# One transformer step on a Trainium2 core: the first modulation alone at the front, and attention's addend made from the second norm's result

## The chip, the core and the metric

The kernel runs on one core of one Trainium2 chip. Its engines are TensorE (PE in the profile, with PEld for its weight loads), VectorE (DVE), ScalarE (ACT), GpSimd (POOL) and SyncE (SP), which issues most DMAs. The metric is the device time of one execution in microseconds (us). Everything is float32.

## The reference

The input x is 16 sequences of 128 tokens with 128 features. Four residual sublayers follow one another: an adaptive-norm transformer block (self-attention, cross-attention to a context of 77 tokens, a gated feed-forward), a mixture of experts with a shared expert, a slot attention of three turns, and a second mixture of experts. Each sublayer gets a plain layer norm of the running sum and is added to it. The change touches the start of the first sublayer alone:

```python
def adaln(x, t, w, b):
    emb = t @ w + b
    scale, shift = jnp.split(emb, 2, axis=-1)
    return layernorm(x) * (1.0 + scale) + shift
...
h1 = adaln(x, t, norm1_w, norm1_b)
x = mha(h1, h1, attn1_wq, attn1_wk, attn1_wv, attn1_wo, attn1_bo) + x
h2 = adaln(x, t, norm2_w, norm2_b)
x = mha(h2, context, attn2_wq, attn2_wk, attn2_wv, attn2_wo, attn2_bo) + x
h3 = adaln(x, t, norm3_w, norm3_b)
x = glu_ff(h3, ff_w1, ff_b1, ff_w2, ff_b2) + x
```

The x of this block is already layernorm(x) of the input, so h1 needs the norm of a norm. With v the variance of the input, the first norm divides by sqrt(v + eps), and the norm of that divides x - mean by sqrt(v(1 + eps) + eps^2). Both come from one set of statistics. t is one vector per sequence (cond), so there are 16 scales and 16 shifts for each of the three norms: the three modulations.

## The kernel before, in words

All sixteen sequences stay in SBUF: x0 is the input, r the running sum of the first sublayer, each 128 tokens on the partitions by 16 x 128. Attention works in groups of two sequences: groups 0 to 7 are self-attention, 8 to 15 cross-attention. The code is written in program order; a scheduler then sets the order of the instructions on each engine, and each engine runs its own list in that order. An instruction that waits holds everything behind it on its engine.

The loads (lines 111 to 125) are all issued from SP's queue in the order of the code: the first two sequences of x0, the columns of biases (cols_sb), condT, normw (the weights of all three modulations, 384 KB), the two weights of self-attention (wa0 for query and key, wa1 for value and output), the rows of biases spread over all partitions (brow, srow), the other x0 in seven loads, the context, and the rest. From the ninth load on, a load also waits on SP for the one eight places before it.

The modulations (lines 152 to 157) come first in the code: per norm, two matmuls of a 128x128 block of normw with condT into a PSUM tile pe, and two DVE instructions that make ada_sc (1 + scale) and ada_sh (shift).

attn_norm (line 250) makes a group's norm. For self-attention: variance (statistics sti, and the small steps dmi, qqi, mvi on 128x2), two small DVE steps that write the two variances into q (lines 261 and 262, tile qjj), POOL's power to -0.5 (rsqrt, line 170, tile yj), and then normalize (line 217) twice, two DVE instructions each: z (tile za) for the attention, and r, the plain norm of x, which is the addend of the residual. At last POOL adds the output bias to r (row_add, line 244, from brow). z has two buffers, the small tiles six each; r has a place of its own for every sequence and waits for none.

attn_prologue (line 272) transposes z on PE (ta), has ACT apply the modulation (ha, line 281), and projects queries, keys (pq, line 298, copied by ACT at line 299) and values (pv, line 314). scores (line 339) multiplies queries by keys for eight heads into a PSUM tile s of which there are two buffers, and on DVE takes the maximum (mx, line 363), subtracts it (e, line 365, which frees the buffer), on ACT the exponential, on DVE the sum and its reciprocal (lines 368 and 369), and on POOL the multiplication by it (line 370). attend_t transposes e (te, line 380), attend_v multiplies it with the values, attn_project applies the output weights (ya) and adds the result into r (line 404). The loop over units (one sequence of one group each) starts the next group's prologue before a group's first unit, and runs a unit's scores one unit ahead. The projections of a group and its values use the same two PSUM buffers (psM, tag "mm") as the modulations.

Of the kernel before, what the change touches and what calls it, by code (L numbers as in the profile page):

```python
# [14 lines left out]
ALU = mybir.AluOpType  # L15
# [3 lines left out]
P = 128  # L19
B = 16  # L20
D = 128
# [8 lines left out]
LN_EPS = 1e-5  # L30
# [26 lines left out]
def pixart_kernel(  # L57
# [18 lines left out]
    V, S, G, PE = nc.vector, nc.scalar, nc.gpsimd, nc.tensor  # L76
# [15 lines left out]
    normw = attc.tile([P, 6, D], F32, name="normw")  # L92
    ctxT = attc.tile([P, B * NC], F32, name="ctxT")
    brow = const.tile([P, 9, D], F32, name="brow")
# [7 lines left out]
    dma = nc.sync.dma_start  # L102
# [3 lines left out]
    def load_w(src, n, name):  # L106
        t = wpool.tile([P, n], F32, name=name, tag="w")
        dma(out=t, in_=src)
        return t
# [1 line left out]
    dma(out=x0[:, 0:2, :], in_=xr[:, 0:2, :])  # L111
    dma(out=cols_sb, in_=cols)
    dma(out=condT, in_=cond_t)
    dma(out=normw, in_=norm_w.rearrange("p (k d) -> p k d", d=D))
    w_att = [load_w(attn_w[0], 2048, "wa0"), load_w(attn_w[1], 2048, "wa1")]
    dma(out=brow, in_=rows[0, 0 : 9 * D].partition_broadcast(P).rearrange("p (k d) -> p k d", d=D))
    dma(out=srow, in_=rows[0, R_SMALL * D : N_ROWS].partition_broadcast(P))
    for b in range(2, B, 2):
        dma(out=x0[:, b : b + 2, :], in_=xr[:, b : b + 2, :])
    dma(out=ctxT, in_=ctx_feat)  # L120
    w_att += [load_w(attn_w[2], 2048, "wa2"), load_w(attn_w[3], 2048, "wa3")]
# [24 lines left out]
    def col(i, p=P):  # L146
        return cols_sb[:p, i : i + 1]
# [1 line left out]

    ada_sc = const.tile([P, 3, B], F32, name="ada_sc")  # L150
    ada_sh = const.tile([P, 3, B], F32, name="ada_sh")
    for k in range(3):
        pe = psM.tile([P, 2, B], F32, name=f"ada{k}", tag="mm")
        for j in range(2):
            PE.matmul(pe[:, j, :], lhsT=normw[:, 2 * k + j, :], rhs=condT, start=True, stop=True)
        V.tensor_scalar(ada_sc[:, k, :], pe[:, 0, :], col(C_NORM + 2 * k), 1.0, ALU.add, ALU.add)
        V.tensor_scalar(ada_sh[:, k, :], pe[:, 1, :], col(C_NORM + 2 * k + 1), None, ALU.add)
# [5 lines left out]
    def small(nm, tag, p, n, lane):  # L163

        return sm.tile([P, 4], F32, name=f"{tag}{nm}", tag=f"{tag}{lane}", bufs=6 if lane == "" else 2)[:p, :n]

    def rsqrt(v, p, n, nm, lane):

        y = small(nm, "y", p, n, lane)
        G.tensor_tensor(y, v, mhalf[:p, :n], ALU.pow)  # L170
        return y
# [43 lines left out]
    def normalize(dst, src, rs, mean, n):  # L215
        for i in range(n):
            V.tensor_scalar(
                dst[:, i, :], src[:, i, :], mean[:, i : i + 1], rs[:, i : i + 1], ALU.subtract, ALU.mult
            )
# [15 lines left out]
    def transpose_n(z, p, n, nm, g=0):  # L235

        t = psT.tile([P, 4, P], F32, name=f"t{nm}", tag=t_tag(g))
        for i in range(n):
            PE.transpose(t[:, i, :p], z[:, i, :], ident[:p, :p])
        return t  # L240

    def row_add(ap, k, n):

        G.tensor_tensor(ap, ap, brow[:, k, :].unsqueeze(1).to_broadcast([P, n, D]), ALU.add)


    GB = 2
    GT = GB * P

    def attn_norm(g):  # L250

        ph, gi = divmod(g, B // GB)
        b0 = gi * GB
        rg = r[:, b0 : b0 + GB, :]
        z = zp.tile([P, 4, D], F32, name=f"za{g}", tag="z")
        if ph == 0:

            xg = x0[:, b0 : b0 + GB, :]
            v, mean = variance(xg, P, GB, f"i{g}")
            q = small(f"j{g}", "qj", P, 4, "")  # L260
            V.tensor_scalar(q[:, GB:], v, 1.0 + LN_EPS, LN_EPS * LN_EPS, ALU.mult, ALU.add)
            V.tensor_scalar(q[:, :GB], v, LN_EPS, None, ALU.add)
            rs = rsqrt(q, P, 2 * GB, f"j{g}", "")
            normalize(z, xg, rs[:, GB:], mean, GB)
            normalize(rg, xg, rs, mean, GB)
        else:
            rs, mean = ln_stats(rg, P, GB, f"j{g}")
            normalize(z, rg, rs, mean, GB)
        row_add(rg, R_BO1 if ph == 0 else R_BO2, GB)
        return z  # L270

    def attn_prologue(g, ap_):
        ph, gi = divmod(g, B // GB)
        b0 = gi * GB
        rg = r[:, b0 : b0 + GB, :]
        z = attn_norm(g)
        t = transpose_n(z, P, GB, f"a{g}")
        hT = zp.tile([P, 512], F32, name=f"ha{g}", tag="h")
        for i in range(GB):
            b = b0 + i  # L280
            S.activation(  # L281
                hT[:, i * P : (i + 1) * P], t[:, i, :], AF.Identity,
                bias=ada_sh[:, ph, b : b + 1], scale=ada_sc[:, ph, b : b + 1],
            )
        hT = hT[:, :GT]
        nk = P if ph == 0 else NC
        kvT = hT if ph == 0 else ctxT[:, b0 * NC : (b0 + GB) * NC]
        wqk, wvo = w_att[2 * ph], w_att[2 * ph + 1]
        v = ap_.tile([P, GB, H, DH], F32, name=f"v{g}", tag="v")
        if ph == 0:  # L290
            qT = ap_.tile([P, 8, GT], F32, name=f"q{g}", tag="q")
            kT = ap_.tile([P, 8, GT], F32, name=f"k{g}", tag="k")
            for dst, src, w0, n in ((qT, hT, 0, GT), (kT, kvT, 1024, GB * nk)):
                for c in range(0, 8, 2):
                    pq = psM.tile([P, 2, 256], F32, name=f"pq{g}_{w0}_{c}", tag="mm")
                    for j in range(2):
                        w = w0 + (c + j) * P
                        PE.matmul(pq[:, j, :n], lhsT=wqk[:, w : w + P], rhs=src, start=True, stop=True)  # L298
                    S.copy(dst[:, c : c + 2, :n], pq[:, :, :n])  # L299
        else:  # L300

            qT = hT
            kT = ap_.tile([P, H, GB * NC], F32, name=f"k{g}", tag="k")
            for c in range(0, H, 3):
                m = min(3, H - c)
                pq = psM.tile([P, 3, GB * NC], F32, name=f"pk{g}_{c}", tag="mm")
                for j in range(m):
                    w = (c + j) * D
                    PE.matmul(pq[:, j, :], lhsT=wqk[:, w : w + D], rhs=kvT, start=True, stop=True)  # L309
                S.copy(kT[:, c : c + m, :], pq[:, :m, :])  # L310
        for i in range(GB):
            for hh in range(2):
                pv = psM.tile([P, 8, DH], F32, name=f"pv{g}_{i}_{hh}", tag="mm")
                PE.matmul(  # L314
                    pv[:nk].rearrange("p h d -> p (h d)"), lhsT=kvT[:, i * nk : (i + 1) * nk],
                    rhs=wvo[:, hh * 512 : (hh + 1) * 512], start=True, stop=True,
                )
                S.copy(v[:nk, i, hh * 8 : (hh + 1) * 8, :], pv[:nk])  # L318
        return dict(ph=ph, b0=b0, nk=nk, qT=qT, kT=kT, v=v, wo=wvo, g=g)
# [121 lines left out]
    ap_ = att_ctx.enter_context(tc.tile_pool(name="att", bufs=2))  # L441
    if True:
        units = [(g, i) for g in range(NG) for i in range(GB)]
        states = {0: attn_prologue(0, ap_)}
        e_next = [scores(states[0], 0, hg, ap_) for hg in range(2)]
        late = None
        glu_h = {}
        for n, (g, i) in enumerate(units):
            if n in (8, 9):
                fold(w_att[2], n - 8)  # L450
            if i == 0:
                if g + 1 < NG:
                    states[g + 1] = attn_prologue(g + 1, ap_)
                else:
                    glu_h[0] = glu_prologue(0)
            e = e_next
            more = n + 1 < len(units)
            if more:
                g1, i1 = units[n + 1]
                e_next = [None, None]  # L460
            oT = ap_.tile([P, 8, P], F32, name=f"oT{g}_{i}", tag="oT")
            eT = [None, None]
            if more:
                e_next[0] = scores(states[g1], i1, 0, ap_)
            eT[0] = attend_t(states[g], i, 0, e[0], ap_)
            if late:
                attn_project(*late)
            if more:
                e_next[1] = scores(states[g1], i1, 1, ap_)
            eT[1] = attend_t(states[g], i, 1, e[1], ap_)  # L470
            attend_v(states[g], i, 0, eT[0], oT)
            attend_v(states[g], i, 1, eT[1], oT)
            late = (states[g], i, oT)
        attn_project(*late)
# [12 lines left out]
    def wide(nm):  # L487
        return psS.tile([P, 512], F32, name=nm, tag="s")

    ph = ctx.enter_context(tc.tile_pool(name="ph", bufs=2))  # L490
# [7 lines left out]
        out=cb,  # L498
        in_=rows[0, R_COND * D : (R_COND + B) * D].partition_broadcast(P).rearrange("p (b d) -> p b d", d=D),
# [32 lines left out]
    def router(i, zT, w0, ne, bias0, nm):  # L532
# [11 lines left out]
        out=before, in_=before, compare_op=ALU.is_gt, fill=0.0, base=0, pattern=[[1, P]], channel_multiplier=-1  # L544
# [673 lines left out]
```

## Time and profile before

| What | us |
|---|---|
| Median of nine runs | 933.39 |
| Lowest and highest of them | 929.05 and 940.19 |
| The profiled execution | 939.74 |
| Its span in the profile | 938.0 |
| Busy in the span: PE, DVE, ACT, POOL | 818.1, 634.1, 409.5, 367.4 |
| Mean granted clock of TensorE | 0.93 |

Times in the profile are counted from the start of the span. A line of a timeline has the start, the length, the engine, the source line, the operation, the tiles written and read, and in brackets the idle time of the engine before it and what ended it. "x2" is two instructions merged into one line. A line of a chain of waits has the start, the length and the step that held the end at that time. A line of the windows has a stretch, and in it the busy time of PE, PEld, DVE, ACT and POOL, each with its number of instructions, the granted clock, the share of the DMA engines in use and their GB/s. Granted clock is the part of its clock that TensorE was given; at 0.50 a matmul takes about twice as long. Source lines are those of the kernel before.

### The profile page before, as it was taken

Reading aid. Unit: us, or ns where it says so; the run is one execution under the profiler, and the core shown is the slowest. Engines: PE = TensorE matmul, PEld = TensorE weight load, DVE = VectorE, ACT = ScalarE, POOL = GpSimd, SP = SyncE. Lnnn points to the kernel's source line nnn. Section 1 sums busy time; section 2 is a strip of 40 time slices with the busy share of each in tenths; the row PEclk is TensorE's granted clock in tenths of the full one; section 3 lists DMA queues with packets and bytes.
Section 4 is the critical chain, followed back from the end, with each engine's and each line's share of the span. In section 5 each row is a group of like instructions: output and inputs, shape, how many; then the busy total and the mean of one; then the engine's idle time right before and its main releaser. Section 6 shows DMA issues by size and latency. Waiting matters only on the chain.

```text
span 938.0 us, 16193 instructions
## 1 busy us (share of the span) xinstructions
PE 818.1 (87%) x5803; PEld 647.8 (69%) x5803; DVE 634.1 (68%) x1900; ACT 409.5 (44%) x859; POOL 367.4 (39%) x408
## 2 busy tenths in 40 slices
PE   6699999999999999999999969999558778684696
PEld 4477777777777887777766549988446556563586
DVE  4796666866766666666877865655677677768454
ACT  3345555445554444444422203443046666651242
POOL 3432232223332222223442046775254354542576
PEclk9799999999999999999999988999569898976799
DMA  8100000000000000000200146994200000002894
GB/s 326 47 1 1 2 1 1 1 1 2 1 1 1 1 1 1 1 1 1 71 3 24 57 146 193 332 308 170 84 0 1 1 1 2 12 23 57 270 339 149
DMA packets 29419, 61.82 MB, mean 66 GB/s; under 512 B 4250, under 2 KB 17901, under 8 KB 28699
## 3 DMA queue, kind: packets, MB, share of 16 engines
q1 hardware_dynamic: 25067, 51.70, 16.2%
q0 software_dynamic: 4272, 9.09, 3.3%
q8 instruction: 46, 0.75, 0.3%
q14 instruction: 34, 0.28, 0.1%
HBM read 54.01 MB, written 7.23 MB: 65 GB/s over the span
## 4 chain that ended last, share of the span: by engine, by line
PE 55%; DVE 24%; POOL 8%; DMA 6%; ACT 3%; issue 3%; SPq 0%; POOLq 0%; ACTq 0%; DVEq 0%
PE pv L314 6%; PE po L390 5%; PE pq L298 5%; PE ya L400 4%; PE gum L813 4%; PE te L380 4%; PE pk L309 4%; PE s L346 4%; DVE mx L363 3%; DVE e L365 2%; PE ynm L824 2%; DMA zsn<-tok,frmn 2%; PE h1n L1057 2%; DMA res<-ysm,tom 2%; DVE ri L368 2%
## 5 line engine op out<-in xcount | busy, mean ns | idle before, releaser
L370 POOL TENSOR_TENSOR e<-e,ri 128x1024 f32<-128x1024 f32 (+1 forms) x64 | 100.4, 1568 | 228.3 <-DVE ri L369 175.2
L363 DVE TENSOR_REDUCE mx<-s 128x8 f32<-128x1024 f32 (+1 forms) x64 | 64.3, 1004 | 27.9 <-PE s L355 21.5
L366 ACT ACTIVATE e<-e 128x1024 f32<-128x1024 f32 (+1 forms) x64 | 57.1, 892 | 52.5 <-DVE e L365 52.3
L368 DVE TENSOR_REDUCE ri<-e 128x8 f32<-128x1024 f32 (+1 forms) x64 | 64.2, 1004 | 20.2 <-ACT e L366 19.9
L381 DVE COPY eT<-te 128x512 f32<-128x512 f32 (+1 forms) x64 | 43.4, 678 | 50.3 <-PE te L380 49.8
L380 PE MATMUL te<-ident,e 128*128 128x128 f32 (+1 forms) x512 | 71.7, 276 | 4.8 <-POOL e L370 4.7
L390 PE MATMUL po<-eT,v 128*64 128x128 f32 (+1 forms) x1024 | 75.3, 279 | 0.5 <-DVE eT L381 0.3
L381 ACT COPY eT<-te 128x512 f32<-128x512 f32 (+1 forms) x64 | 37.4, 584 | 86.3 <-PE te L380 85.7
L380 PEld LDWEIGHTS te<-ident,e 128*128 128x128 f32 (+1 forms) x512 | 59.2, 144 | 20.8 <-issue 6.8
L390 PEld LDWEIGHTS po<-eT,v 128*64 128x64 f32 (+1 forms) x1024 | 60.7, 136 | 15.5 <-DVE eT L381 8.6
L298 PE MATMUL pq<-ha,wa 128*128 128x256 f32 x256 | 66.7, 411 | 1.4 <-ACT ha L281 0.9
L365 DVE TENSOR_TENSOR e<-s,mx 128x1024 f32<-128x1024 f32 (+1 forms) x64 | 64.5, 1007 | 2.3 <-POOL e L370 0.5
L400 PE MATMUL ya<-wa,oT 128*128 128x128 f32 x512 | 63.1, 276 | 0.0
L813 PE MATMUL gum<-zTnm,wm 128*128 128x128 f32 x456 | 61.3, 275 | 0.0
L400 PEld LDWEIGHTS ya<-wa,oT 128*128 128x128 f32 x512 | 59.8, 192 | 1.1 <-ACT v L318 0.6
L298 PEld LDWEIGHTS pq<-ha,wa 128*128 128x128 f32 x256 | 47.8, 201 | 14.4 <-ACT q L299 2.4
L813 PEld LDWEIGHTS gum<-zTnm,wm 128*128 128x128 f32 x456 | 56.8, 192 | 0.2
L355 PE MATMUL s<-k,q 64*128 64x128 f32 x512 | 44.0, 290 | 8.2 <-DVE e L365 8.2
L714 POOL DMA_INDIRECT zsm<-tok,frmm x38 | 36.8, 969 | 34.4 <-DVE secm L692 21.2
L355 PEld LDWEIGHTS s<-k,q 64*128 64x128 f32 x512 | 34.8, 187 | 18.7 <-issue 15.7
L318 ACT COPY v<-pv 128x512 f32<-128x512 f32 (+1 forms) x64 | 37.3, 584 | 19.3 <-PE pv L314 19.3
L735 POOL DMA_INDIRECT res<-ysm,tom x38 | 37.4, 983 | 16.8 <-ACT ysm L828 6.9
(378 smaller groups left out, 1881.5 us busy)
## 6 DMA issues: line engine op xcount, KB each, us to landing
wm<-in_moe_w_dram SPq DMA_DIRECT2D x38, 576.0 KB, 5.3
wn<-in_moe_w_dram SPq DMA_DIRECT2D x23, 578.0 KB, 5.2
wa<-in_attn_w_dram SPq DMA_DIRECT2D x4, 1024.0 KB, 7.5
ygm<-res SPq DMA_DIRECT2D x8, 256.0 KB, 2.7
tok<-stm SPq DMA_DIRECT2D x4, 258.0 KB, 2.9
tok<-stn SPq DMA_DIRECT2D x4, 258.0 KB, 4.2
x<-in_x_dram SPq DMA_DIRECT2D x8, 128.0 KB, 8.8
cb<-in_rows_dram SPq DMA_DIRECT2D x1, 1024.0 KB, 9.2
```

What stands on the lines that cost most here:

```text
L298: PE.matmul(pq[:, j, :n], lhsT=wqk[:, w : w + P], rhs=src, start=True, stop=True)
L355: PE.matmul(ps[:, par, j * nk : (j + 1) * nk], lhsT=st["qT"][h0 : h0 + DH, c, i * P : (i + 1) * P], rhs=st["kT"][h0 : h0 + DH, c, i * nk : ...
L363: V.tensor_reduce(mx, pv, AX.X, ALU.max)
L365: V.tensor_tensor(e, pv, mx.unsqueeze(3).to_broadcast([P, 2, 4, nk]), ALU.subtract)
L366: S.activation(e, e, AF.Exp, scale=1.0 / math.sqrt(DH))
L368: V.tensor_reduce(ri, e, AX.X, ALU.add)
L370: G.tensor_tensor(e, e, ri.unsqueeze(3).to_broadcast([P, 2, 4, nk]), ALU.mult)
L380: PE.transpose(t[:nk, j, :], e[:, par, j, :], ident)
L381: (S.copy if par == 0 else V.tensor_copy)(eT[:nk, par], t[:nk])
L390: PE.matmul(po[par * DH : (par + 1) * DH, j, :], lhsT=st["v"][:nk, i, 8 * hg + 2 * j + par, :], rhs=eT[:nk, par, j, :], start=True, stop=True,
L400: PE.matmul(y, lhsT=oT[:, c, :], rhs=st["wo"][:, 1024 + c * D : 1024 + (c + 1) * D], start=(c == 0), stop=(c == 7),)
L813: PE.matmul(ps[j][:, c * P : (c + 1) * P], lhsT=w[:, k : k + P], rhs=zT, start=True, stop=True)
```

## The change

normw is loaded in two parts: the 128 KB of the first modulation at the old place, the 256 KB of the other two behind the second load of x0. The three modulations become a function adaln(k). The norm of group 0 (attn_norm) now stands first in the code, then adaln(0), then the prologue of group 0, then adaln(1) and adaln(2).

For self-attention, r is no longer made from x but from z. With y1 and y2 the two reciprocal roots, w = (v(1 + eps) + eps^2) * y2 * y1 is y1 / y2, so that z * w is the plain norm of x. The two multiplications that make w run on POOL on 128x2 elements. The output bias is added in the same DVE instruction that multiplies z by w, so POOL's row addition is left to cross-attention alone. r of a group thus waits for that group's z, which has two buffers, and for brow.

```diff
-    dma(out=normw, in_=norm_w.rearrange("p (k d) -> p k d", d=D))
+    nw = norm_w.rearrange("p (k d) -> p k d", d=D)
+    dma(out=normw[:, 0:2, :], in_=nw[:, 0:2, :])
...
     for b in range(2, B, 2):
+        if b == 4:
+            dma(out=normw[:, 2:6, :], in_=nw[:, 2:6, :])
         dma(out=x0[:, b : b + 2, :], in_=xr[:, b : b + 2, :])
...
-    for k in range(3):
+    def adaln(k):
         pe = psM.tile([P, 2, B], F32, name=f"ada{k}", tag="mm")
...
             q = small(f"j{g}", "qj", P, 4, "")
-            V.tensor_scalar(q[:, GB:], v, 1.0 + LN_EPS, LN_EPS * LN_EPS, ALU.mult, ALU.add)
+            w = q[:, GB:]
             V.tensor_scalar(q[:, :GB], v, LN_EPS, None, ALU.add)
-            rs = rsqrt(q, P, 2 * GB, f"j{g}", "")
-            normalize(z, xg, rs[:, GB:], mean, GB)
-            normalize(rg, xg, rs, mean, GB)
+            V.tensor_scalar(w, v, 1.0 + LN_EPS, LN_EPS * LN_EPS, ALU.mult, ALU.add)
+            y = rsqrt(q, P, 2 * GB, f"j{g}", "")
+
+            G.tensor_tensor(w, w, y[:, GB:], ALU.mult)
+            G.tensor_tensor(w, w, y[:, :GB], ALU.mult)
+            normalize(z, xg, y[:, GB:], mean, GB)
+            for i in range(GB):
+                V.scalar_tensor_tensor(
+                    rg[:, i, :], z[:, i, :], w[:, i : i + 1], brow[:, R_BO1, :], ALU.mult, ALU.add
+                )
         else:
             rs, mean = ln_stats(rg, P, GB, f"j{g}")
             normalize(z, rg, rs, mean, GB)
-        row_add(rg, R_BO1 if ph == 0 else R_BO2, GB)
+            row_add(rg, R_BO2, GB)
         return z
...
-        z = attn_norm(g)
+        z = z0 if g == 0 else attn_norm(g)
...
+        z0 = attn_norm(0)
+        adaln(0)
         states = {0: attn_prologue(0, ap_)}
+        adaln(1)
+        adaln(2)
```

## The prediction

> **What bounds the kernel now.** I read the page's engine shares and slices first (PE 87% busy, nines in nearly every slice up to the twentieth), then the timeline of the first 40 us, since everything the change touches stands there, then the chain of waits in that stretch, then the windows for the granted clock. After 34 us the first attention phase is PE's: from 34 to 240 us PE's gaps over 0.1 us add up to only 5.2 us. So time won before 34 us stays won, if nothing new is put in PE's way later. PE's timeline has the one large gap of the phase:
>
> ```profile
> 23.44 2.06 PE L355 MATMUL s<-k,q 64*128 64x128 f32 x32
> 25.43 0.44 PE L239 MATMUL ta<-ident,za 128*128 128x128 f32 x2
> 33.24 0.76 PE L355 MATMUL s<-k,q 64*128 64x128 f32 x2 [7.37 <-DVE e L365]
> 33.93 0.79 PE L298 MATMUL pq<-ha,wa 128*128 128x256 f32 x1
> ```
>
> PE ended the first two score tiles at 25.5 and the next group's transposes at 25.87. Its next instruction needs a score buffer that DVE frees with the subtraction e at L365, and group 1's projections (pq) are queued behind it. DVE gets there late, as the chain of waits shows in order of time (start, length, step):
>
> ```profile
> 4.66 9.00 DMA x<-in_x_dram
> 13.69 0.50 DVE sti L204 x2
> ...
> 22.12 1.03 POOL yj L170
> 23.17 0.60 DVE r L217 x2
> 23.84 0.08 DVE mvi L212
> 23.92 0.20 DVE sti L204
> 24.12 0.49 DVE qjj L261
> ...
> 30.55 1.13 DVE mx L363
> 31.68 0.28 DVE r L217
> 31.96 1.14 DVE e L365
> 33.10 0.14 issue
> ```
>
> The scores are ready at 24.6, but DVE works through norms of groups 1 to 7 from 13.69 to 30.48. Two kinds of loss stretch that work, here of one group in DVE's and POOL's timelines:
>
> ```profile
> 23.17 0.60 DVE L217 TENSOR_SCALAR r<-x,mvi,yj 128x128 f32<-128x128 f32 x2 [0.73 <-POOL yj L170]
> 24.03 0.57 DVE L261 TENSOR_SCALAR qjj<-qqi 128x2 f32<-128x2 f32 x1
> 24.80 0.16 DVE L209 SCALAR_TENSOR_TENSOR dmi<-dmi 128x2 f32<-128x2 f32 x1
> ...
> 23.86 0.73 POOL L244 TENSOR_TENSOR r<-r,brow 128x256 f32<-128x256 f32 x1 [0.72 <-DVE qqi L210]
> 24.75 1.02 POOL L170 TENSOR_TENSOR yj<-qjj,mhalf 128x4 f32<-128x4 f32 x1 [0.17 <-DVE dmi L207]
> ```
>
> The r pair waits for POOL's power (0.73 us of idle), and then POOL's row addition of 0.73 us holds a DVE instruction of 0.15 us for 0.57 us. The gap also costs clock:
>
> ```profile
> 25.00:30.00 5.00, 0.87 (x12) 0.51 (x8) 3.45 (x17) 0.81 (x2) 3.24 (x4) 0.83 0.25 93
> 30.00:35.00 5.00, 1.76 (x5) 1.39 (x6) 5.00 (x13) 1.06 (x1) 1.02 (x1) 0.50 0.02 3
> 35.00:40.00 5.00, 5.00 (x16) 3.96 (x15) 5.00 (x11) 2.11 (x4) 2.63 (x2) 0.65 0.00 0
> ```
>
> The last figures of a line are granted clock, DMA share and GB/s. In windows of 1 us the clock is 1.00 until 28, 0.50 from 29 to 38 and 1.00 from 39.
>
> **The change part by part.** *The front, PE.* normw (384 KB) is issued at 2.29 and lands 3.1 us later; PE's first modulation matmul is at 5.57, and z of group 0 (za) waits on DVE behind all three modulations until 8.61. The 128 KB left in its place should land like x's first 128 KB, 2.3 us after issue: at 4.6 (bounds 4.2, by condT's 1.9 us, and 5.4, nothing won). From the first matmul to the first modulation's second DVE step and za are 0.14 + 1.04 + 0.29 us by the rows of before, so za starts at 6.05 (POOL's power is done at 5.64): 2.55 us earlier. The projections move from 10.63 to 8.1; wa0 does not hold them, since the fifth of the seven later x loads, which waits for it on SP's queue, went out at 8.13, and 256 KB fewer now go before it (at the 407 GB/s of the window from 5 to 10 us, 0.64 us). The first score tile, done at 24.6, then ends at 22.0, plus 0.9 for the two modulations now ahead of its end (8 passes; 0.215 us apart in the cold clock of before, half of that here): 22.9. Their PSUM buffers come free by ACT's v copies, and group 1's projections wait for DVE to read them, both in time.
>
> *The loads.* On SP's queue the second normw load goes behind the second x load; wa, brow and that x load have 256 KB less ahead, the later x loads none. So x of group 1 lands at 13.05 (before 13.69), at worst where it did. A load more also shifts the queue's turns: each later x load waits for one load earlier in line; DVE reads them at 15 us or later.
>
> *Group 0's addend.* r is now made on DVE, at its place in line, and waits for brow. That landed 9.0 us after 3.71, at 12.7, so now about 12.1. Two instructions end at 12.7, and group 1's statistics, queued behind, have no data before 13.05: hidden. A brow later than 12.45 would hold DVE by the excess.
>
> *DVE from 13.05 to the first reduction.* In the built order all statistics of groups 1 to 7 still stand ahead of the reduction, but only r of groups 1 and 2. Group 1: statistics 1.36 us (group 0: 3.08 to 4.44), 0.15 to POOL, power 1.02, so za at 15.6; two za and two r take 1.04 (16.40 to 17.43): 16.65. POOL's two new multiplications stand between power and r; 128x4 ones take 0.2 us (L185, L194), so they are done at about 16.05, when r comes up at 16.1. Group 2: three statistics at 0.205 us and eight small steps at 0.072 (starts in the stretch from 21.4 to 22.4) give 1.2, then 0.15, 1.02 and 1.04: 20.1. What remains is 7 statistics and 36 small steps without a wait for POOL: 1.4 + 2.6, and 0.3 for steps that depend on the one just before: 24.4. Four modulation steps at 0.15 and 0.1 for POOL's small multiplications: **25.1** against 30.48. The bounds: 24.7 without the last two allowances; 28.0 if x gains nothing (0.6) and 12 multiplications of 0.2 us each hold DVE for all their time as L244 does (2.4, of which 0.1 is counted). The rows lie near the low end: a hold lasts as long as POOL's instruction moves data, and 128x2 is a hundredth of 128x256.
> The reduction and e follow (1.13 + 1.22 + 0.14; before, an r of 0.28 stood between): PE resumes at 27.6 instead of 33.24, **5.64 us** earlier.
>
> *The clock.* Matmuls of the pq kind start 0.43 us apart at 0.50 and 0.216 at 1.00; 33.24 to 38.5 at half clock lost 2.6 us. The new gap, from 23.8 + 0.4 to 27.6, is 3.4 us instead of 7.4. The half clock began 2.8 us after PE stopped and ended 5.3 after it resumed. The clock's steps here are 3.4 us or a multiple of it, so I take one spell of 3.4 us, which loses 1.7: **0.9 us** won. Bounds: 2.6 (no drop), and a loss of 0.8 (two spells). The Trainium skill, "TensorE: Matmul & The Clock Gate", What's actually happening, says that the gate judges free-running windows of 3.4 us; the trace agrees: half clock from about 28.3 to 38.5, three times 3.4 us. By that rule a gap of 3.4 us fills one window or is split over two, so one spell, the 0.9 us above, would be the usual case and none the rare one.
>
> *What comes later instead.* r of groups 3 to 7 (two instructions, 0.6 us a group) goes onto DVE inside the attention units. A row with the same operands, L924 with brow, takes 0.34 us but up to 1.37 behind a POOL addition; here POOL's e multiplication (L370, 1.90 us) starts just as the r of groups 5 and 6 come up. So the price is 0 to 1.9 us a group, 9.5 in all. I take **0.2** in all: in these places DVE idles before its next dependent step (74 to 80.5, 103.3 to 108.2, 156.3 to 166.8) while PE projects. POOL's eight row additions vanish; it idles anyway. Beyond this, PE and ACT change order only in two groups, where one transposes later; total work there is the same, so zero, within 0.5 either way by the 0.7 us gaps at "te".
>
> Sum: 5.64 + 0.9 - 0.2 = 6.3 us. The profiled execution took 939.74 (span 938.0) and would take 933.4; the median, 933.39, lies 6.35 lower, a difference outside the parts touched, so the forecast is **927.1**.
>
> **The rivals.** *The norms still run ahead.* All eight groups' statistics and powers do stand ahead of the reduction. If POOL's multiplications hold DVE in full and x lands as before, the reduction starts at 28.0, PE resumes 2.7 us earlier instead of 5.64, and with the clock's 0.9 and the 0.2 the gain is 3.4: **930.0**. For it: the 0.57 and 0.69 us rows. Against it: these rows lie under 128x256 additions.
> *The power holds DVE.* If DVE instructions with two SBUF inputs stop for all of POOL's power, groups 3 to 7 lose up to 0.9 each: 4.5, gain 1.8: **931.6**. The row at 24.80 speaks against it: 0.16 us, begun 0.05 us into a power of 1.02. The Trainium skill, "SBUF — State Buffer", Who interferes with whom, says that such a DVE instruction and a GpSimd instruction that reads SBUF exclude each other, the second waiting for the first. By that rule this rival would hold; the trace agrees under L244 and disagrees under L170.
> *Slower: the late addends.* If all five r pairs wait for POOL's e multiplication and nothing hides it, 9.5 - 6.5 = 3.0 us slower: **936.4**. It decides once PE loses more than 1.3 us a group. For it: the placement next to L370; against: DVE's idle spells.
> *More: the clock never drops.* The gap misses its window: 5.64 + 2.6 - 0.2 = 8.0: **925.4**.
>
> **How the numbers follow.** Medians of nine runs between 929 and 940 tell about 0.5% (4.7 us) from no change. Chances: forecast 0.55, statistics still ahead 0.17, power 0.06, late addends 0.10, no clock drop 0.12. Faster by over 0.5% means under 928.7: most of the forecast (0.45), the clock case (0.11) and a part of the first rival (0.08), 0.64. Slower than 938.1: the late addends with an unlucky run, 0.08. Between: 0.28. The range, 921.5 to 933.0, takes in the bounds of the gap, clock and runs, leaving out the late addends and the outer tails.
>
> **What would show it.** Right: the first reduction starts at 25 +- 1, PE's gap behind the first scores falls to 3 to 4 us, pq of group 0 starts near 8.1, no row of 0.57 or 0.69 among the norms' small steps, PE's gaps up to 240 us unchanged but for an equal shift. Wrong: first reduction beyond 28, L170 over small steps of 0.5 us or more, r rows near 1.9 us with a PE gap behind them, or an equal front but a later stage longer by as much.

## The result, and the profile after

The changed kernel takes 928.75 us (median of 18 runs, 924.7 to 933.22); the kernel before, run beside it, 935.18 us (55 runs, 929.05 to 941.85). The ratio is 0.9932 with a 95% interval of 0.9914 to 0.995: 6.4 us, or 0.7%, faster. The prediction was a gain of 6.3 us and 927.1 us, with 921.5 to 933.0 as its range. The profiled execution of the changed kernel took 929.29 us, its span 927.6.

First PE's timeline of the changed kernel, the counterpart of the rows that opened the prediction:

```profile
4.60 1.01 PE L158 MATMUL ada<-condT,normw 128*128 128x16 f32 x4 [4.60 <-DMA normw<-in_norm_w_dram]
6.33 0.73 PE L242 MATMUL ta<-ident,za 128*128 128x128 f32 x2 [0.72 <-DVE za L220]
7.96 8.82 PE L308 MATMUL pq<-ha,wa 128*128 128x256 f32 x32 [0.90 <-ACT ha L291]
...
23.61 0.44 PE L242 MATMUL ta<-ident,za 128*128 128x128 f32 x2
27.55 0.49 PE L365 MATMUL s<-k,q 64*128 64x128 f32 x4 [3.50 <-DVE e L375]
27.97 6.31 PE L308 MATMUL pq<-ha,wa 128*128 128x256 f32 x20
```

The projections start at 7.96 instead of 10.63. PE resumes behind the first scores at 27.55 instead of 33.24, and its gap is 3.50 us instead of 7.37. The chain of waits shows why it still waits that long:

```profile
12.55 0.61 DVE r L273 x2
13.17 0.50 DVE sti L207 x2
...
19.70 0.61 DVE r L273 x2
20.39 0.08 DVE mvi L215
20.47 0.19 DVE sti L207
...
24.87 0.14 DVE ada_sh L160
25.01 1.14 DVE mx L373
26.18 1.23 DVE e L375
```

All statistics still stand ahead of the first reduction, but r of groups 3 to 5 is gone from there, and so are three of the five waits for POOL's power (the r that stood between the first reduction and e before is gone too). The second kind of loss, POOL's row addition holding DVE, is gone as well, as DVE's and POOL's timelines show around a power:

```profile
20.85 0.16 DVE L214 TENSOR_TENSOR mvi<-sti 128x2 f32<-128x2 f32 x1
20.88 1.01 POOL L173 TENSOR_TENSOR yj<-qjj,mhalf 128x4 f32<-128x4 f32 x1 [1.21 <-DVE dmi L210]
20.92 0.17 DVE L212 SCALAR_TENSOR_TENSOR dmi<-dmi 128x2 f32<-128x2 f32 x1
```

The small steps take 0.15 to 0.17 us under the power; the rows of 0.57 and 0.69 us are gone with the row addition. By the rows, DVE's line between x of group 1 and the first reduction is rid of 2.3 us of waits for the power, 2.3 us of holds and 1.6 us of r itself, and has 0.6 us of modulation steps more. No run separates these parts of the gain.

**How the traces are compared.** Two rows of PE serve as milestones: the transposes te that wait 0.40 us for POOL (57.26 us in the kernel before) and the ones that wait 0.70 us (148.83). How much earlier a kernel reaches such a row is its lead. The changed kernel reaches them at 50.49 and 142.70: leads of 6.77 and 6.13. From there to the gated feed-forward's last tiles near 504 us the lead stays at 6.1. The rows, of the kernel before and then of the changed one:

```profile
57.26 1.09 PE L380 MATMUL te<-ident,e 128*128 128x128 f32 x8 [0.40 <-POOL e L370]
...
148.83 1.09 PE L380 MATMUL te<-ident,e 128*128 128x128 f32 x8 [0.70 <-POOL e L370]
```

```profile
50.49 1.09 PE L390 MATMUL te<-ident,e 128*128 128x128 f32 x8 [0.40 <-POOL e L380]
...
142.70 1.09 PE L390 MATMUL te<-ident,e 128*128 128x128 f32 x8 [0.70 <-POOL e L380]
```

Behind 510 us, in the mixtures of experts, executions of one kernel differ by several us, which is why the lead tells kernels apart that the times do not.

### The profile page after: what moved, and what is told of

It is laid out like the page before. It is cut to its first block, busy times and chain, and to the rows that moved or that the text cites. A ratio compares the mean times of both kernels' runs of the same rounds, so it can differ in the third digit from the quotient of the medians.

```text
span 927.6 us, 16205 instructions
## 1 busy us (share of the span) xinstructions
PE 812.1 (88%) x5803; PEld 643.4 (69%) x5803; DVE 634.0 (68%) x1900; ACT 408.6 (44%) x859; POOL 364.2 (39%) x416
## 4 chain that ended last, share of the span: by engine, by line
PE 55%; DVE 23%; POOL 8%; DMA 6%; issue 3%; ACT 3%; SPq 0%; POOLq 0%; ACTq 0%; DVEq 0%
PE pv L324 6%; PE po L400 5%; PE pq L308 5%; PE ya L410 5%; PE te L390 4%; PE gum L827 4%; PE pk L319 4%; PE s L356 4%; DVE mx L373 3%; DMA zsn<-tok,frmn 2%; PE ynm L838 2%; DVE e L375 2%; DMA res<-ysm,tom 2%; PE h1n L1071 2%; POOL ym L173 2%
```

## The experiments

They ran on chips on which the kernel before took 977.47, 978.98 and 974.02 us; the extra 40 us come behind 510 us, and the ratios are against runs on the same chip. Restart is the start of PE's first score row behind its gap; half clock after it shows in the 20 rows of projections (pq) that follow, 4.74 us at full clock. The clock's part is the first lead less what the restart gained.

| Kernel | Restart | Gap | Half clock after it | First lead | Clock's part | Second lead | Ratio (95%) |
|---|---|---|---|---|---|---|---|
| before | 33.24 | 7.37 | yes | | | | |
| changed | 27.55 | 3.50 | yes | 6.77 | 1.08 | 6.13 | 0.9932 (0.9914 to 0.995) |
| changed again | 27.57 | 2.07 | no | 8.30 | 2.63 | 7.64 | 0.9925 (0.9886 to 0.9964) |
| changed, third | 27.90 | 2.40 | no | 7.98 | 2.64 | 7.32 | 0.9925 (0.9895 to 0.9955) |
| front alone | 34.73 | 9.87 | yes | -1.15 | 0.34 | -0.81 | 1.0009 (0.9987 to 1.0032) |
| addend alone | 27.05 | 1.43 | no | 8.83 | 2.64 | 8.17 | 0.992 (0.989 to 0.995) |
| addend alone again | 27.79 | 2.14 | no | 8.09 | 2.64 | 7.43 | 0.9884 (0.9861 to 0.9907) |
| one load | 28.00 | 1.53 | no | 7.88 | 2.64 | 7.22 | 0.992 (0.989 to 0.9949) |
| addend twice | 27.59 | 3.29 | yes | 6.68 | 1.03 | 6.03 | 0.9928 (0.9902 to 0.9955) |
| PE kept busy | 27.50 | 0.52 | no | 7.13 | | 6.47 | 0.9931 (0.9905 to 0.9957) |
| one buffer | 26.66 | 1.41 | no | 9.22 | 2.64 | 8.56 | 0.9908 (0.9882 to 0.9934) |
| one buffer again | 26.92 | 1.40 | yes | 7.35 | 1.03 | 6.70 | 0.9898 (0.9873 to 0.9923) |
| addend, one buffer | 27.53 | 1.41 | no | 8.35 | 2.64 | 7.68 | 0.9903 (0.9878 to 0.9929) |
| warm front, one buffer | 25.42 | 2.00 | no | 10.46 | 2.64 | 9.80 | 0.9896 (0.9868 to 0.9924) |

The first leads consist of two terms: what the restart gained, and 2.64 us where no half clock follows it, 1.0 to 1.1 where one spell of 3.4 us does. In the row "PE kept busy" this does not hold, and with the front alone the half clock lasts 10.2 us, as before, and the second term is 0.34. Between the two milestones every kernel with the new addend loses 0.64 to 0.67 us.

**Which half of the change does it.** The theory: DVE's line of norms ahead of the first reduction sets PE's restart. The rival: PE's earlier start at the front carries through. First the front alone:

```diff
-            G.tensor_tensor(w, w, y[:, GB:], ALU.mult)
-            G.tensor_tensor(w, w, y[:, :GB], ALU.mult)
-            normalize(z, xg, y[:, GB:], mean, GB)
-            for i in range(GB):
-                V.scalar_tensor_tensor(rg[:, i, :], z[:, i, :], w[:, i : i + 1], brow[:, R_BO1, :], ...)
+            normalize(z, xg, rs[:, GB:], mean, GB)
+            normalize(rg, xg, rs, mean, GB)
...
+        row_add(rg, R_BO1 if ph == 0 else R_BO2, GB)
```

> The front as in the changed kernel (first modulation alone, normw in two loads), the addend made the old way: two normalizations and POOL's row addition. Theory (DVE's work ahead of the first reduction sets PE's restart, so PE's earlier start is waiting time gained at the wrong end): all r of groups 1 to 7 stand ahead of the first reduction again, 14 instead of before's 12, and four modulation steps of 0.14 us besides. Before, DVE needed 16.8 us from x of group 1 to the reduction (13.69 to 30.48); with 2 r more (0.57) and the four steps (0.57) it is 17.9 from 13.1, so the reduction starts at 31.0, PE resumes at 33.6 and its gap is over 9 us; time like before, 0.4 us over it (935.6, within 1.5). Rival (PE's head start of 2.6 us at the front carries through): the reduction at 28, PE resumes near 30.6, 2.6 us under before (932.6).

Measured: ratio 1.0009, no difference by time; by the trace 0.8 us slower. DVE's timeline of this kernel (its r is L220, its reduction L366) and then PE's:

```profile
28.26 0.60 DVE L220 TENSOR_SCALAR r<-x,mvi,yj 128x128 f32<-128x128 f32 x2 [0.73 <-POOL yj L173]
31.58 0.60 DVE L220 TENSOR_SCALAR r<-x,mvi,yj 128x128 f32<-128x128 f32 x2 [0.92 <-POOL yj L173]
32.09 1.22 DVE L366 TENSOR_REDUCE mx<-s 128x8 f32<-128x1024 f32 x1
```

```profile
24.42 0.44 PE L242 MATMUL ta<-ident,za 128*128 128x128 f32 x2
34.73 0.76 PE L358 MATMUL s<-k,q 64*128 64x128 f32 x2 [9.87 <-DVE e L368]
```

PE was through a microsecond sooner and waited 2.5 us longer. The expectation had the reduction at 31.0 and it came at 32.09: one more r pair was counted there, but not the wait of 0.92 us for POOL ahead of it. The rival falls. Now the addend alone:

```diff
-    dma(out=normw[:, 0:2, :], in_=nw[:, 0:2, :])
+    dma(out=normw, in_=norm_w.rearrange("p (k d) -> p k d", d=D))
...
-        z = z0 if g == 0 else attn_norm(g)
+        z = attn_norm(g)
```

> The kernel before with the new addend alone; front and loads as before. Theory: after x of group 1 (13.69 us) DVE has the changed kernel's work, 11.2 us there from 13.17 to 24.36, without the four modulation steps, which are done early: the first reduction starts at 24.9, just behind the scores that end at 24.6, and PE resumes at 27.5, as in the changed kernel. PE ends its earlier work at 26.1, so its gap is only 1.4 to 1.7 us; if that lets the clock stay at full, this kernel gains the 1.7 us that one spell of half clock costs the changed kernel: 8 us under before, 927, 1.5 us under the changed kernel. Rival (the front gives a part of the gain of its own, up to its 2.6 us): PE resumes near 30, 3.8 us under before (931.4). Rival (clock drops all the same): 928.8, level with the changed kernel.

Measured: ratio 0.992, second lead 8.17, against 6.13 of the changed kernel's first execution.

```profile
25.18 0.44 PE L239 MATMUL ta<-ident,za 128*128 128x128 f32 x2
27.05 0.49 PE L362 MATMUL s<-k,q 64*128 64x128 f32 x4 [1.43 <-DVE e L372]
27.47 4.74 PE L305 MATMUL pq<-ha,wa 128*128 128x256 f32 x20
```

The restart is 0.5 us earlier than the changed kernel's, and the 20 rows of projections run at full clock: 4.74 against 6.31 us. So the new addend brings the whole gain, and the front added to it brought nothing: it starts PE earlier, and PE waits the longer for DVE. The repetition asked whether that execution was a lucky one.

> The new addend alone on the front of before, again. Theory: the scores, ending between 24.3 and 24.9 by where the clock's windows lie, set the reduction; PE resumes at 27.0 to 27.5 behind a gap of 1.4 us, the clock stays at full, lead 7.7 to 8.2 after 140 us; so over several runs level with the changed kernel or up to 1 us faster. Rival (the lead of 8.2 was one lucky execution): a lead under 7, half clock behind the gap.

Measured: lead 7.43 and ratio 0.9884, 962.93 us against 965.66 for the changed kernel on the same chip. Restart (27.79) and gap (2.14) lie over what was expected, since here DVE and not the scores came last: x of group 1 kept it waiting until 14.23, and the reduction started at 25.17. The addend alone is at least level with the changed kernel; that it is faster the times do not settle, as the intervals overlap.

**The split load.** All of normw in one load, in the place of the changed kernel's two:

> The changed kernel with all of normw (384 KB) in one load at the front, as before. Theory: x of group 1 lands at 13.7 instead of 13.1 and DVE's line of norms shifts by it, the first reduction from 24.9 to 25.4 or 25.5 and PE's restart from 27.55 to 28.1; PE starts its first modulation 1 us later (5.6), and that is hidden in its gap, which shrinks to about 3 us. So 0.5 us over the changed kernel by the trace up to 240 us, 929.3, with one or no spell of half clock (1.7 us less). Rival (the early start of PE counts): 1 us over the changed kernel or more, 929.8, and PE's restart at 28.6. Rival (the split load is worth nothing, x of group 1 does not move): level with it.

Measured: restart 28.00, 0.45 later than the changed kernel's, as the theory had it, and a gap of only 1.53, behind which the clock stays at full. So the lead is 7.22, more than the 6.13 of the changed kernel's first execution and close to its other two (7.64, 7.32). One execution does not tell 0.45 us, as the changed kernel's own restarts spread by 0.35. But over all executions the statistics of group 1 start at 13.02 to 13.53 with the split load and at 13.44 to 14.23 with one load. So x of group 1 comes about 0.5 us earlier, and behind PE's gap that is all that can be seen of the split load.

**The late addends.**

```diff
-            for i in range(GB):
+            for i in [i for i in range(GB) for _ in range(2 if g >= 3 else 1)]:
```

> The changed kernel with the addend of groups 3 to 7 written twice: ten more DVE instructions of 0.27 to 0.34 us inside the attention units, same result. The lead over before falls in the traces from 6.8 us at 47 us to 6.1 after 140 us; the theory puts these 0.7 us on the five late pairs. If what they cost is DVE's time in the way of the next reductions, ten more cost another 0.7 (lead 5.4 after 140 us, 929.5 in all). If every r of these groups is exposed in full, 10 times 0.3, 3 us (lead 3.1, 931.7). Rival (DVE idles in these places, or POOL's e multiplication is what holds the first r of a pair and the second finds POOL done): no change, lead 6.1, 928.8; then the 0.7 us come from the hold or from PE's changed order.

Measured: second lead 6.03 against 6.13, so DVE's own time for r costs nothing: ten more instructions moved it by 0.1. What the pairs do cost is a hold, and the trace of the changed kernel has the place (several engines' timelines):

```profile
62.01 1.90 POOL L380 TENSOR_TENSOR e<-e,ri 128x1024 f32<-128x1024 f32 x1 [2.34 <-PE te L390]
62.85 1.20 DVE L273 SCALAR_TENSOR_TENSOR r<-za,qjj,brow 128x128 f32<-128x128 f32 x1
63.97 1.21 DVE L375 TENSOR_TENSOR e<-s,mx 128x1024 f32<-128x1024 f32 x1
...
65.22 1.06 ACT L376 ACTIVATE e<-e 128x1024 f32<-128x1024 f32 x1 [0.82 <-DVE e L375]
66.18 1.05 ACT L309 COPY k<-pq 128x512 f32<-128x512 f32 x2
66.80 1.99 PE L308 MATMUL pq<-ha,wa 128*128 128x256 f32 x8 [0.47 <-ACT k L309]
```

r comes up under POOL's e multiplication and lasts 1.20 us instead of 0.34; e behind it, ACT's exponential behind e and ACT's copies of the keys behind that are late, and PE idles 0.47 us for a projection buffer. With the addend the old way (front alone), the same projections go on without a gap:

```profile
70.97 1.21 DVE L368 TENSOR_TENSOR e<-s,mx 128x1024 f32<-128x1024 f32 x1
72.22 1.06 ACT L369 ACTIVATE e<-e 128x1024 f32<-128x1024 f32 x1
73.17 1.07 ACT L302 COPY k<-pq 128x512 f32<-128x512 f32 x2
...
74.18 1.99 PE L301 MATMUL pq<-ha,wa 128*128 128x256 f32 x8
```

DVE's timeline of the doubled kernel at the same place:

```profile
62.94 1.20 DVE L273 SCALAR_TENSOR_TENSOR r<-za,qjj,brow 128x128 f32<-128x128 f32 x1
64.06 1.21 DVE L375 TENSOR_TENSOR e<-s,mx 128x1024 f32<-128x1024 f32 x1
65.20 0.59 DVE L273 SCALAR_TENSOR_TENSOR r<-za,qjj,brow 128x128 f32<-128x128 f32 x2
```

The first r lasts 1.20 again and those behind it, which find POOL done, 0.3 each; PE's gap is 0.47 again, as in every kernel with the new addend. That is most of the 0.64 us by which the changed kernel's lead falls between the milestones; the rest was not followed up.

**The half clock.** Is it the gap? Group 1's two transposes were issued eight times each, to fill it:

```diff
-        for i in range(n):
+        for i in [i for i in range(n) for _ in range(8 if nm == "a1" else 1)]:
```

> The changed kernel with each of group 1's two transposes issued 8 times into the same place (same result, 14 passes of 0.22 us more, 3.0 us): PE's gap before its restart at 27.55 is filled up to about 27.1 us with work that nothing needs. Theory (a gap of over 3 us costs the half clock, one spell of 3.4 us, 1.7 us): the clock stays at full, the lead over before in the trace after 140 us is 7.6 to 7.8 instead of 6.1; ACT reads the transposes later, which may cost 0.2 of it. Rival (the half clock follows something else, or the passes come in the way): lead 6.1 or less. Against the time of before: 7.7 us less by the theory, 6.1 by the rival.

Measured: no half clock, but a second lead of only 6.47. The 16 transposes took 1.97 us and not 3.0 and more, and ACT could apply the modulation only after the exponential that had come up meanwhile, so group 1's projections waited another 0.98 us. A filled gap keeps the clock here; it says nothing on gaps, though, because the changed kernel itself showed both. Its repetitions:

> The changed kernel itself, for a comparison on the chip of these runs: lead 6.1 in the trace after 140 us, half clock for one spell of 3.4 us behind the gap, 6 to 6.5 us under before. A spell more or less, by where the clock's windows lie, would show as 1.7 us.

> The changed kernel a third time. Two executions of it in the traces differ: in one the clock rose at 10.85 us, the first scores ended early, PE's gap was 3.5 us and half clock followed (lead 6.1 after 140 us); in the other it rose at 13.33, the gap was 2.1 and none followed (lead 7.6). Theory (the clock's windows stand differently in each execution; restart of PE at 27.55 in both, set by DVE): restart at 27.5 to 27.6 again, lead 6.1 with a rise before 11.5 us and 7.6 with a later one, nothing between or beyond by more than 0.3. Rival (something else differs between the executions): another restart or lead.

Measured: no half clock in either (second leads 7.64 and 7.32). PE's timeline of the first of them:

```profile
25.06 0.44 PE L242 MATMUL ta<-ident,za 128*128 128x128 f32 x2
27.57 0.49 PE L365 MATMUL s<-k,q 64*128 64x128 f32 x4 [2.07 <-DVE e L375]
28.00 4.74 PE L308 MATMUL pq<-ha,wa 128*128 128x256 f32 x20
```

The restart is DVE's and hardly moves (27.55 to 27.90; in the third, DVE waited for x of group 1 until 13.50 instead of 13.17). What moves is when PE is done: 23.61 for the transposes in one execution, 25.06 in the two others. The 32 rows of group 0's projections started at 7.96 and took 8.82 us in the first, at 8.41 and 9.75 us in the second, at 8.94 and 9.22 us in the third: they begin at half clock, and how long they stay there differs (the trace's first record of the clock, its rise to full, is at 10.85, 13.33 and 12.79 us). An execution whose scores are early does not resume earlier. It only has the longer gap: 3.50 us here and 3.29 in the kernel with the addend twice (transposes at 23.61 and 23.85), both with half clock behind it, so these two end up later.

**A shorter line on DVE.** If the later of DVE's line and of the scores sets the restart, then with less on DVE the front should begin to pay. One buffer each for the first norms' small tiles keeps the statistics of groups 5 to 7 from running ahead:

```diff
-        return sm.tile([P, 4], F32, name=f"{tag}{nm}", tag=f"{tag}{lane}", bufs=6 if lane == "" else 2)[:p, :n]
+        return sm.tile([P, 4], F32, name=f"{tag}{nm}", tag=f"{tag}{lane}", bufs={'': 6, 'i': 1}.get(lane, 2))[:p, :n]
...
-        st = sm.tile([P, 4, 6], F32, name=f"st{nm}", tag="st")[:p, :n, :]
+        st = sm.tile([P, 4, 6], F32, name=f"st{nm}", tag="sti", bufs=1)[:p, :n, :]
...
-        dm, mean, q = (small(nm, k, p, n, "") for k in ("dm", "mv", "qq"))
+        dm, mean, q = (small(nm, k, p, n, "i") for k in ("dm", "mv", "qq"))
```

> The changed kernel with own small tiles for the first norms, one buffer each instead of six, so that statistics of groups 5 to 7 (6 statistics and about 30 small steps, 1.2 + 2.1 us) no longer stand ahead of the first reduction. Theory (the later of DVE's line and of the scores sets PE's restart): DVE is through at 21.6, so the scores' end at 22.5 decides, the reduction starts at 22.5 and PE resumes at 25.1 instead of 27.55; the gap is 1.1 us, the clock stays at full: 2.45 + 1.7 = 4.1 us more, lead 10.2 in the trace after 140 us. The front's earlier start pays here. Rival (the statistics and powers cost their time where they stand now, inside the attention units): up to 3.3 us given back after 30 us, lead 6.9.

> The new addend alone on the front of before, with the same one buffer for the first norms' small tiles. Theory (the later of two): DVE is through 3 us earlier, but the scores end at 24.4 as with the addend alone, so the reduction stays there and the lead after 140 us stays 8.2; 2 us less than with the new front, which is what the front is worth once DVE is not the last. Rival (DVE's line alone decides, the front is worth nothing): lead 10.

> The changed kernel with one buffer for the first norms' small tiles, again. Theory: the scores set the reduction, 22.5 with an early rise of the clock (10.9 us), 24.0 with one at 12.6 as seen; PE resumes at 25.1 to 26.7 behind a gap of 1.4 us, no half clock, lead 8.5 to 10.2 after 140 us. Rival: a lead under 8.

DVE's timelines of the first two, with the changed front and with the front of before:

```profile
24.03 1.23 DVE L373 TENSOR_REDUCE mx<-s 128x8 f32<-128x1024 f32 x1 [0.48 <-PE s L365]
```

```profile
24.90 1.23 DVE L370 TENSOR_REDUCE mx<-s 128x8 f32<-128x1024 f32 x1 [2.99 <-PE s L362]
```

In both DVE now waits for the scores, as the theory says, and the statistics cost nothing where they stand now (the leads fall by 0.66 and 0.67 between the milestones, as without them). With the front of before nothing was won over the addend alone (second lead 7.68 against 8.17 and 7.43). With the changed front the restart is at 26.66 and 26.92, 0.6 to 0.9 us before the 27.53 of the old front and not the 2 us that were expected, because the scores ended at 24.0 and 24.3 instead of 22.5. The repetition also had half clock behind a gap of 1.40 us:

```profile
26.92 0.49 PE L365 MATMUL s<-k,q 64*128 64x128 f32 x4 [1.40 <-DVE e L375]
27.34 6.35 PE L308 MATMUL pq<-ha,wa 128*128 128x256 f32 x20
```

while gaps of 1.41 to 2.40 us in eight other executions had none.

**Where the front's head start goes.** PE was kept busy on zeros ahead of its first projections:

```diff
+    def keep_busy(ps, n):
+        for _ in range(n):
+            PE.matmul(ps, lhsT=zero_sb, rhs=zero_sb, start=True, stop=True)
...
+        if k == 0:
+            keep_busy(pe.rearrange("p a b -> p (a b)"), 8)
...
+        if nm == "a0":
+            keep_busy(t[:, 0, :], 2)
         for i in range(n):
             PE.transpose(t[:, i, :p], z[:, i, :], ident[:p, :p])
+        if nm == "a0":
+            keep_busy(t[:, 3, :], 2)
```

> As the kernel with one buffer, and PE kept busy at the front by twelve 128x128 passes on zeros that nothing reads: eight ahead of the first modulation (from 1.3 us), two ahead of group 0's transposes and two behind them; they fill PE's waits for normw, z and ACT. Theory (PE's early projections run at half clock until the first window of 3.4 us that PE works through, so most of the front's head start is lost there): the clock rises by 8 us instead of 10.9 to 13.3, the projections of group 0 (32 in 9.3 us before) take about 7 us, the scores end at 21.5 to 22, DVE is through at about 22, PE resumes at 24.5 to 25: lead 10.2 to 10.8 after 140 us. Rival (the rise follows something else than PE's work): rise at 10.9 to 13.3 as before, lead 8.5 or less, with the passes in the way.

```profile
1.32 3.78 PE L157 MATMUL ada<-zero_sb 128*128 128x128 f32 x16 [1.32 <-POOL zero_sb L143]
...
8.68 7.41 PE L318 MATMUL pq<-ha,wa 128*128 128x256 f32 x32 [1.21 <-ACT ha L301]
...
25.42 0.49 PE L375 MATMUL s<-k,q 64*128 64x128 f32 x4 [2.00 <-DVE e L385]
```

The clock's rise stands at 6.65 us in this trace, and at 10.85 to 13.99 in the eight executions with the changed front as it is. The 32 rows of projections take 7.41 us instead of 8.82 to 10.31, the restart comes at 25.42 and the second lead is 9.80, the largest of all and just under what the theory gave (10.2). DVE came last again: its reduction started at 22.80, right behind the modulation steps. The restart is 1.2 to 1.5 us ahead of the two with one buffer (26.66 and 26.92). So in this one execution a part of the front's early start came back that projections at half clock had taken. By time this kernel (0.9896, 964.35 us), the one-buffer kernel (0.9898, 963.81) and the addend alone (0.9884, 962.93) cannot be told apart, nor any of them from the changed kernel beside them (0.9925, 965.66) beyond the overlap of their intervals: leads that differ by 3 us drown in the later stages' spread.

## Why the prediction was right, point by point

*The front, PE.* First modulation at 4.6, za at 6.05, projections at 8.1 predicted; 4.60, 5.94 and 7.96 in the profiled execution. In the repetitions the first modulation came at 5.05 and 5.58, the second of them past the bound of 5.4 at which the smaller load wins nothing, and the projections began at 8.41 and 8.94.

*The loads and group 0's addend.* x of group 1 was expected at 13.05 and its statistics began at 13.17, right behind the two r at 12.55, which waited for brow (expected at 12.1). They started 0.1 us past the 12.45 named as the bound and so took 0.1 us from DVE at most.

*DVE to the first reduction.* 25.1 predicted, 24.93 measured: group 1's za at 15.65 (15.6), the end of group 2's r at 20.3 (20.1), no instruction held by the new multiplications.

*The restart.* 27.6 and 5.64 us earlier predicted, 27.55 and 5.69 measured.

*The clock.* One spell, 0.9 us, predicted; 1.08 in the profiled execution. But the case "the clock never drops", given a chance of 0.12, held in the changed kernel's two repetitions (2.63 and 2.64, where the prediction had 2.6). The step that failed is the claim that one spell "would be the usual case and none the rare one". The gap was taken as 3.4 us; with later scores it is 2.1 to 2.4. Nor does one spell follow from a gap of 3.4 us by the prediction's own words, since such a gap, split over two windows, fills neither; and a gap of 1.40 us had a spell behind it in one execution. The size of a spell was right: 1.6 us measured (2.64 less 1.03 to 1.08) for the 1.7 taken. The 2.8 us from PE's stop to the half clock are read from the scores' end at 25.5; from the transposes' end at 25.87 they are 2.4, and nothing in the sum hangs on it. The Trainium skill, "TensorE: Matmul & The Clock Gate", What's actually happening, also says that the start of full clock depends on where the free-running window stands when the first matmul comes; the spread of 8.82 to 10.31 us for the same 32 rows of projections in eight executions with the changed front agrees. The prediction drew on the window for the gap and left it out for the front, where it decides how long the gap is.

*The late addends.* 0.2 us predicted, 0.47 shown at one place, 0.64 at most. The step that failed is "in these places DVE idles before its next dependent step". Two of the five pairs were not held (0.56 us for both instructions, groups 5 and 6), two were held at no visible cost (2.25 and 2.00 us, groups 3 and 7), but at group 4 a subtraction (e) stood right behind r, and the hold behind POOL's e multiplication, which the prediction named with up to 1.9 us, went through ACT to PE. The prediction expected that hold at groups 5 and 6, the two that were not held. The term is mis-sized, not missed.

*The rivals.* "The norms still run ahead" was right that all statistics do, wrong that they would be held: no row over 0.3 us among them. "The power holds DVE" fell: 0.17 us under it. The rule cited there from the Trainium skill, "SBUF — State Buffer", Who interferes with whom, again agrees at one place and not at another: r with its two SBUF inputs is held by POOL's e multiplication (1.20 us for 0.34), the small steps are not by its power. "Slower: the late addends" needed 1.3 us of PE's time per group and got 0.47 in one.

*The sum.* 5.64 + 0.9 - 0.2 = 6.3 predicted; 5.69 + 1.08 - 0.64 = 6.1 in the profiled execution, 7.6 and 7.3 in the two others, 6.4 by the medians. That the medians meet the sum within 0.1 us is in part luck: single executions lie between 6.1 and 7.6, and the clock's part and the late addends were off in opposite directions. The forecast of 927.1 is 1.65 under the measured median because it started from a median of 933.39, which over 55 runs is 935.18.

What the sum hid is that its terms came from one half of the change. The front moved PE by 2.7 us, and in the sum that figure appears only as a longer gap; the 0.5 us that DVE won by the earlier x is paid back by the four modulation steps of 0.14 us that now stand ahead of the reduction. The experiments made that plain: the front alone was worth -0.8 us and the addend alone the whole gain.

## What to carry to other kernels

Where two engines meet, an edit on the one that comes first buys idle time; price each half of a change at the meeting point by the engine that comes last there, and expect the other half to begin to pay only once that line is shorter. Instructions that a scheduler lets run ahead are not free because nobody waits for them: they stand in front of the one that somebody does wait for, and what is moved out of that line is better put where no large POOL instruction with the same kind of operands runs. For differences of a few us in a long kernel, compare the start of the same row in two traces rather than two medians, and look at more than one execution of the kernel itself before an explanation rests on one.

## What had not been expected of the hardware

The same kernel, with the same order of instructions, ran its first 32 rows of projections in 8.82, 9.75 and 9.22 us and was left with a gap of 3.50, 2.07 or 2.40 us, with half clock behind it or not: 1.5 us of lead between executions from the clock alone. A gap's length does not settle it: 1.40 us had a spell of half clock behind it, 2.40 us had none. By the clock's records every spell at this place lasts 3.41 or 10.24 us and begins 13.65 or 17.07 us, a whole number of 3.41, behind the rise. PE's busy time in the 3.41 us ahead does not settle it either: 2.01 us in the execution with the spell behind 1.40 us (24.24 to 27.65), and less, 1.68 us, in the same place (the fourth stretch of 3.41 us behind the rise) of an execution without a spell (addend alone again, 23.97 to 27.38). What decides it stays open. And the half pace at the front is not in the column of the granted clock. Two windows of the changed kernel (PE's busy time with its rows first, the granted clock third from the end):

```profile
8.00:10.00 2.00, 2.00 (x5) 1.64 (x6) 0.00 (x0) 0.00 (x0) 0.00 (x0) 1.00 0.98 409
...
12.00:14.00 2.00, 2.00 (x11) 1.51 (x10) 1.41 (x8) 1.17 (x2) 0.00 (x0) 1.00 1.07 335
```

PE is busy throughout both and does 5 rows in the one and 11 in the other, and both read 1.00. The first record of the clock in this trace is the rise at 10.85 us, so ahead of it the 1.00 stands for no record.
